# Fetching a layer's sub-weights by computed row numbers, and spreading a norm's statistics over four slots

## The chip, the cores and the metric

The kernel runs on one core of one Trainium2 chip. The metric is the device time of one execution in microseconds (us), the median of several runs. All values are fp32. The engines are named as the profile names them: PE is TensorE's matmuls and PEld its weight loads, DVE is VectorE, ACT is ScalarE, POOL is GpSimd, SP is the sync engine.

## The reference, cut to what matters

Each of 16 images (256 channels of 28 x 28) is group-normed, goes through two convolutions that are replaced by a lookup, and is added to itself.

```python
def amm_conv3x3(x, centroids, w_sub):                 # centroids (256,16,9), w_sub (256,9,256)
    p = patches(x)                                    # (B, 784, 256, 9)
    d = |p|^2 - 2 p.centroids + |centroids|^2         # (B, 784, 256, 16)
    attn = softmax(-d)
    lut = einsum('cks,cso->cko', centroids, w_sub)
    return einsum('bnck,cko->bno', attn, lut)

def block(v):
    out = relu(bn(amm_conv3x3(v, centroids1, wsub1)))
    out = bn(amm_conv3x3(out, centroids2, wsub2))
    return relu(se_layer(out) + v)

x = x + block(group_norm(x, G=32))                    # statistics over 8 channels x 784 points
```

The norm of an image is needed before that image's first layer and depends on nothing else, so its place in the program is free within limits. And `wsub2` is a weight: 256 x 9 rows of 256 floats, 2.36 MB, needed once, from layer 2's first tile on.

## The kernel before

The program is 32 stages (16 images, two layers) of 16 tiles, 512 tiles in all. I call the time of one tile a slot. A plan puts each small job (a norm step, a copy, a pattern write) into a slot, with a position within it: `SMALL` is in the middle of TensorE's work, `REST` at the end. Per tile TensorE makes 32 small logits matmuls, 32 small lookup matmuls and 8 or 10 large ones (128x384 or 128x400) with the sub-weights, as the profile counts them: it shows two for every matmul call in the code. VectorE transposes, GpSimd scales, ScalarE takes exponentials.

The kernel sorts channels by a key computed on the chip. `perm` is the sorting as a 0/1 matrix; a product with it on TensorE puts rows in sorted order. The second layer's sub-weights were sorted so, written to DRAM, and copied back in the layout that the large matmuls need:

```python
def load_part(ap, i):                       # 384 columns of wsub2, 393 KB
    t = tpool.tile([P, 832], F32, tag="z", name="part")[:, : NB * PART].rearrange(...)
    nc.sync.dma_start(t, ap[:, i * PART : (i + 1) * PART].rearrange("(b p) m -> p b m", p=P))
    parts[i] = t

def by_position(ps, rhs, m):                # L335: matmuls of 128 x m
    for v in range(NB):
        for b in range(NB):
            nc.tensor.matmul(ps[:, v, :m], lhsT=perm[:, b, v * P : (v + 1) * P], rhs=rhs[:, b],
                             start=(b == 0), stop=(b == NB - 1))

def sort_ws2(i):
    t = parts.pop(i)
    ps = pair()
    by_position(ps, t, PART)
    r = tpool.tile([P, 832], F32, tag="z", name="part")[...]
    nc.vector.tensor_copy(r, ps[:, :, :PART])
    nc.gpsimd.dma_start(view(d_ws2, i * PART, ...), r)

def place_ws2(i, t, j):                     # 16 copies back, and 8 more in place_tail
    p = 32 * i + 16 * t + 8 * j
    nc.sync.dma_start(ws[1][p : p + 8, : 2 * NQ], view(d_ws2, (NRT * j + 4 * t + i) * 9 * C, ...))

# ... in the plan:
for i in range(9 * C // PART):              # six parts
    plan.at(3 + i, REST, load_part, wsub2, i)
    plan.at(4 + i, REST, sort_ws2, i)
moves = [(place_wd2, ...) ...]              # 18 moves of the codes
moves += [(place_cw2, ...) ...]             # 32 moves of the codes
moves += [(place_ws2, ...) ...]             # 16
moves += [(place_tail, ...) ...]            # 8
for i, (f, *a) in enumerate(moves):
    plan.at(6 + i // 3, REST, f, *a)
```

The norm takes six slots: statistics of the image's two halves of channels, a matmul that averages them over each group, GpSimd's squared deviation `dv` of each channel's mean from its group's, a second matmul, and the two apply steps:

```python
def gn_stats(b, k):
    ...
    for i in range(2):
        nc.vector.bn_stats(st[:, i, :], xs[b][:, k, i * (HW // 2) : (i + 1) * (HW // 2)])   # L428
    nc.vector.bn_aggr(gst[b][:, k, :], st)

def gn_mean(b):
    nc.tensor.matmul(ps, lhsT=gmat, rhs=mv..., start=True, stop=True)     # L434
    nc.scalar.copy(gm..., ps)
    nc.gpsimd.tensor_sub(dv, mv[:, :, 0], gm[:, :, 0])
    nc.gpsimd.tensor_mul(dv, dv, dv)                                      # L439

def gn_var(b):
    nc.tensor.matmul(ps, lhsT=gmat, rhs=dv, start=True, stop=True)        # L445
    ...

def norm(self, b, t):
    self.at(t, REST, gn_stats, b, 0)
    self.at(t + 1, REST, gn_stats, b, 1)
    self.at(t + 2, SMALL, gn_mean, b)
    self.at(t + 3, SMALL, gn_var, b)
    self.at(t + 4, REST, gn_apply, b, 0)
    self.at(t + 5, REST, gn_apply, b, 1)

# ... in the plan, t being the first slot of the image's first layer:
n0 = 3 if b == 1 else t - 2 * NS - 3
plan.at(n0 - (4 if b == 1 else 2), REST, load_x, b, x[b])
plan.norm(b, n0)
```

## Time and profile before

| | before |
|---|---|
| median of 3 runs | 2895.39 us (2892.28 to 2902.37) |
| span of the profiled run | 2894.4 us |
| TensorE busy / idle | 2797.8 / 96.6 us |
| start of tile 4, 10, 34 | 60.3, 118.6, 277.6 us |
| tiles 44 to 480 (steady part) | 2350.3 us, 172.5 per two stages |

Where a tile starts is read by counting the logits matmuls in the timeline.

The first line to read is the chain of work that ended last, followed back from the end, as shares of the span by engine (from the page of the kernel before):

```profile
PE 77%; DMA 9%; POOL 6%; issue 4%; DVE 3%; ACT 0%; SPq 0%; POOLq 0%; DVEq 0%; ACTq 0%
```

TensorE carries three quarters of it. The other quarter is what TensorE waited for, and what those engines had waited for before; it is not TensorE's idle time, which is only 96.6 us. The chain leaves the bound engine only where that engine stopped.

One of the stops that come with every image, first on VectorE's timeline, then on TensorE's. The columns are the start, the duration, the engine and line, the operation with its tiles, the number of instructions, and in brackets the idle time before it and what ended it:

```profile
690.97 1.04 DVE L428 BATCH_NORM_STATS2 gn_st<-xt 128x6 f32<-128x392 f32 x2 [1.85 <-DMA xt<-in_x]
...
692.17 1.94 DVE L658 STREAM_TRANSPOSE nt<-pair 128x832 f32<-128x832 f32 x2
```

The other stop, on TensorE and on GpSimd, for another image:

```profile
1216.44 0.93 PE L578 MATMUL pair<-pt,wd 19*32 19x384 f32 x32
...
1221.07 0.38 PE L445 MATMUL pair<-gn_dv,gmat 128*128 128x2 f32 x2 [1.28 <-POOL gn_dv L439]
```

```profile
1220.83 0.19 POOL L439 TENSOR_TENSOR gn_dv<-gn_dv 128x2 f32<-128x2 f32 x1
```

GpSimd gets to the deviation behind its scaling work of that slot and ends it 4.58 us after the slot's first matmul (1216.44 to 1221.02). TensorE was there after 3.35 us. The first line also shows that an undisturbed set of 32 logits matmuls takes 0.93 us.

This is the view of windows (length of the stretch, then busy time and instructions of PE, PEld, DVE, ACT and POOL, then the granted clock, DMA share and GB/s):

```profile
1557.00:1560.60 3.60, 3.60 (x13) 1.85 (x6) 3.10 (x6) 0.84 (x1) 2.40 (x3) 0.54 0.60 215
```

### The profile page before, as it was taken

The numbers are of one execution on the slowest core, as the hardware profiler recorded it, in microseconds if no ns is written. First come the engines' busy times: TensorE is split into PE (matmuls) and PEld (weight loads), VectorE is DVE, ScalarE is ACT, GpSimd is POOL, SyncE is SP. The second block draws the span as 40 slices with busy tenths as digits, with TensorE's granted clock in tenths as the row PEclk, the third lists the DMA queues.
The fourth block names the chain that finished last, engine by engine and source line by source line (L and its number), as shares of the span: only waits on it lengthen the run. The fifth ranks groups of instructions, "written<-read, shape, count | busy, mean of one in ns | idle before, by whom it ended". The sixth has DMA issues, their size and how long they took to land.

```text
span 2894.4 us, 94782 instructions
## 1 busy us (share of the span) xinstructions
PE 2797.8 (97%) x39834; PEld 1105.5 (38%) x39834; DVE 2258.5 (78%) x2770; ACT 1090.3 (38%) x1595; POOL 1766.8 (61%) x2577
## 2 busy tenths in 40 slices
PE   6998999999999999999999999999999999999996
PEld 3433333333333333333333333333333333333332
DVE  4575888787877878788787877878788787878885
ACT  2332343433434343343433434343343434333332
POOL 3564675666756566675656656566665656656653
PEclk9999999999999999999999999999999999999998
DMA  8776878867767676776767767686776767774651
GB/s 230 193 181 173 208 219 207 221 159 212 192 173 200 153 220 173 198 200 154 217 161 202 190 177 191 158 224 163 216 191 163 204 156 215 185 186 119 154 134 57
DMA packets 296643, 530.27 MB, mean 183 GB/s; under 512 B 94240, under 2 KB 251632, under 8 KB 296208
## 3 DMA queue, kind: packets, MB, share of 16 engines
q0 software_dynamic: 51616, 269.48, 34.8%
q1 hardware_dynamic: 244592, 254.65, 34.5%
q8 instruction: 315, 5.16, 0.8%
q14 instruction: 120, 0.98, 0.1%
HBM read 269.96 MB, written 254.05 MB: 181 GB/s over the span
## 4 chain that ended last, share of the span: by engine, by line
PE 77%; DMA 9%; POOL 6%; issue 4%; DVE 3%; ACT 0%; SPq 0%; POOLq 0%; DVEq 0%; ACTq 0%
PE acc L710 49%; PE pair L578 15%; PE pair L646 13%; DMA xt<-in_x 4%; DMA pt<-pat 3%; POOL k L674 2%; POOL total L686 1%; DVE nt L658 1%; POOL pat L479 1%; POOL tail L680 1%; DVE rc L664 1%; DVE gn_st L428 1%; DMA pat<-side 1%; PE pair L335 1%; DMA part<-in_wsub 0%
## 5 line engine op out<-in xcount | busy, mean ns | idle before, releaser
L710 PE MATMUL acc<-q,ws 128*128 128x384 f32 (+1 forms) x4096 | 1648.1, 520 | 2.3 <-ACT y L732 2.3
L674 POOL TENSOR_TENSOR k<-nt,rc 128x832 f32<-128x832 f32 (+1 forms) x512 | 802.5, 1567 | 1079.0 <-DVE rc L664 1058.9
L658 DVE STREAM_TRANSPOSE nt<-pair 128x832 f32<-128x832 f32 (+1 forms) x1024 | 978.9, 994 | 524.6 <-PE pair L646 405.2
L636 ACT ACTIVATE e<-pair 128x800 f32<-128x800 f32 (+1 forms) x1024 | 789.5, 821 | 1414.7 <-PE pair L578 1368.9
L710 PEld LDWEIGHTS acc<-q,ws 128*128 128x128 f32 x4096 | 699.0, 190 | 900.3 <-issue 578.9
L578 PE MATMUL pair<-pt,wd 19*32 19x384 f32 (+2 forms) x18432 | 575.6, 501 | 33.7 <-DVE nt L658 18.1
L692 DVE STREAM_TRANSPOSE q<-k 128x832 f32<-128x832 f32 (+1 forms) x512 | 488.9, 955 | 0.8 <-POOL k L674 0.8
L646 PE MATMUL pair<-e,cw 32*32 32x384 f32 (+1 forms) x16384 | 485.1, 501 | 0.3 <-DVE nt L658 0.2
L664 DVE RECIPROCAL rc<-nt 128x104 f32<-128x104 f32 (+1 forms) x512 | 398.7, 779 | 17.6
L578 PEld LDWEIGHTS pair<-pt,wd 19*32 19x32 f32 (+1 forms) x18432 | 141.7, 103 | 379.0 <-issue 279.4
L680 POOL TENSOR_TENSOR tail<-nt,rc 128x104 f32<-128x104 f32 (+1 forms) x512 | 236.7, 462 | 0.0
L646 PEld LDWEIGHTS pair<-e,cw 32*32 32x32 f32 x16384 | 119.9, 103 | 290.2 <-issue 146.5
L710 PE MATMUL acc<-qt,ws 128*128 128x400 f32 (+1 forms) x512 | 221.9, 515 | 0.0
L686 POOL TENSOR_TENSOR total<-total,nt 128x96 f32<-128x96 f32 (+1 forms) x448 | 197.3, 440 | 0.0
L479 POOL DMA_DIRECT2D pat<-side x274 | 184.4, 673 | 3.4 <-ACT side L468 3.0
L686 POOL TENSOR_TENSOR total<-total,rc 128x96 f32<-128x96 f32 (+1 forms) x448 | 176.3, 394 | 0.0
L710 PEld LDWEIGHTS acc<-qt,ws 128*128 128x128 f32 x512 | 91.9, 192 | 101.1 <-issue 52.8
L602 DVE TENSOR_REDUCE mx<-z 128x48 f32<-128x768 f32 (+1 forms) x128 | 120.6, 942 | 0.0
L597 DVE STREAM_TRANSPOSE z<-pair 128x768 f32<-128x768 f32 (+1 forms) x128 | 118.1, 961 | 0.1
L479 POOL DMA_DIRECT2D pat<-im x136 | 91.8, 675 | 0.0
L732 ACT ACTIVATE y<-acc,bnsh,bnsc 128x384 f32<-128x384 f32 (+1 forms) x64 | 43.4, 678 | 86.9 <-PE acc L710 81.8
L544 POOL TENSOR_TENSOR y<-y,xt 128x392 f32<-128x392 f32 x60 | 65.9, 1099 | 10.4 <-ACT y L540 10.4
(109 smaller groups left out, 738.8 us busy)
## 6 DMA issues: line engine op xcount, KB each, us to landing
pat<-side POOLq DMA_DIRECT2D x232, 588.0 KB, 5.9
pt<-pat SPq DMA_DIRECT2D x1024, 112.5 KB
pt<-pat SPq DMA_DIRECT2D x1024, 108.0 KB
pat<-im POOLq DMA_DIRECT2D x116, 588.0 KB, 6.0
xt<-in_x POOLq DMA_DIRECT2D x32, 784.0 KB, 8.9
out_dram<-y POOLq DMA_DIRECT2D x16, 784.0 KB, 6.3
pat<-side POOLq DMA_DIRECT2D x24, 300.0 KB, 6.2
pat<-side POOLq DMA_DIRECT2D x18, 288.0 KB, 5.5
```

The lines of the kernel that those rows point to most:

```text
L479: eng.dma_start(view(pat, (ROWS * p0 + 9 * k + 3 * dx) * HW + px, [[ROWS * HW, m], [HW, 3], [1, n]]), bass.AP(v.tensor, v.offset, [list(v. ...
L578: nc.tensor.matmul(ps[t // 2][c : c + 32, t % 2, :n], lhsT=wd[l][32 * i : 32 * i + rows, 4 * u["m"] + t, :], rhs=u["pt"][32 * i : 32 * i + ...
L602: nc.vector.tensor_reduce(u["mx"][:, 2 * v : 2 * v + 2].rearrange("p t (j b) -> p t b j", j=2)[:, :, :nb], u["z"].pop(0)[:, : 64 * nb].rea ...
L636: nc.scalar.activation(e[:, :, :n], ps[:, :, :n], AF.Exp, scale=2.0)
L646: nc.tensor.matmul(u["nm"][t // 2][32 * i : 32 * i + 32, t % 2, :n], lhsT=cw[l][c : c + 32, 4 * u["m"] + t, :], rhs=es[t // 2][c : c + 32, ...
L658: nc.vector.transpose(nt[:, :nb, 2 * v : 2 * v + 2].rearrange("p b t r -> p t b r"), ps[:, :, : 32 * nb].rearrange("p t (b r) -> p t b r", ...
L664: nc.vector.reciprocal(rc[:, : 8 * nb], u["nt"][:, :, SUM])
L674: nc.gpsimd.tensor_tensor(q[:, :nb].rearrange("p b (a s) -> p (b a) s", s=8), nt[:, :, :8], rc.unsqueeze(2).to_broadcast([P, 8 * nb, 8]), ...
L680: nc.gpsimd.tensor_tensor(tails[key][:, :nb, 8 * (m % 4) : 8 * (m % 4) + 8], nt[:, :, 8].rearrange("p (b a) -> p b a", a=8), rc.rearrange( ...
L686: nc.gpsimd.tensor_add(t[:, : 8 * nb], t[:, : 8 * nb], v)
L692: nc.vector.transpose(q[:, :, : 32 * nb].rearrange("p h (b r) -> p h b r", r=32), u.pop("k")[:, :nb].rearrange("p b (h r) -> p h b r", h=2),)
L710: nc.tensor.matmul(accs[key][:, :n], lhsT=ws[l][:, 2 * m + h if h < 2 else 2 * NQ + m // 4, o * P : (o + 1) * P], rhs=u["q"][h][:, :n], st ...
```

## The change

The intent has two parts. First, the sub-weights need not be sorted as data. It is enough to know which channel sits at which position; then the rows can be fetched from the input straight to their places. The change sends the channel numbers through the same sorting product as the batch-norm vectors (`order`), spreads them over partitions with four small matmul calls against constant tables (`where`), multiplies by 9 and adds the tap number, and so has a row number for each of 128 partitions and 18 columns (`src`). Eighteen indirect DMAs from GpSimd, one in each of slots 6 to 23, fetch 128 rows of 1 KB each. The six loads, 48 matmuls, six VectorE copies, six stores and 24 copies back are gone.

Second, the norm: an image is loaded four slots ahead of its first statistics, the four statistics come one to a slot, the two small matmuls stand two slots apart. The apply steps keep their slots.

```diff
-    def load_part(ap, i):
-        ...
-    def sort_ws2(i):
-        ...
-    def place_ws2(i, t, j):
-        ...
-    def place_tail(i, j):
-        ...
+    def find_rows():
+        t = wh.pop()                                   # the constant tables, loaded in slot 2
+        stack = t[:, 4 * P : 4 * P + NLT]
+        ps = bank()[:, :NLT]
+        for c0, c1, part in ((0, 2 * NQ, 0), (2 * NQ, NLT, 1)):
+            for b in range(NB):
+                by = small.tile([P, NLT], F32, name="row_by")
+                nc.vector.tensor_scalar_mul(by[:, c0:c1], stack[:, c0:c1], order[:, b : b + 1])
+                nc.tensor.matmul(ps[:, c0:c1], lhsT=t[:, (2 * part + b) * P : (2 * part + b + 1) * P],
+                                 rhs=by[:, c0:c1], start=(b == 0), stop=(b == NB - 1))
+        nc.vector.tensor_scalar(src[:, : 2 * NQ], ps[:, : 2 * NQ], 9.0, t[...], op0=ALU.mult, op1=ALU.add)
+        nc.vector.tensor_scalar(src[:, 2 * NQ :], ps[:, 2 * NQ :], 9.0, 8.0, op0=ALU.mult, op1=ALU.add)
+
+    def fetch_ws2(g):
+        nc.gpsimd.indirect_dma_start(
+            out=ws[1][:, g], out_offset=None, in_=wsub2.rearrange("c (s o) -> (c s) o", s=9),
+            in_offset=bass.IndirectOffsetOnAxis(ap=src[:, g : g + 1], axis=0),
+        )
 # ... norm:
-            self.at(t, REST, gn_stats, b, 0)
-            self.at(t + 1, REST, gn_stats, b, 1)
-            self.at(t + 2, SMALL, gn_mean, b)
-            self.at(t + 3, SMALL, gn_var, b)
-            self.at(t + 4, REST, gn_apply, b, 0)
-            self.at(t + 5, REST, gn_apply, b, 1)
+            for n, (k, i) in enumerate((k, i) for k in range(NB) for i in range(2)):
+                self.at(t - 7 + n, REST, gn_stats, b, k, i)
+            self.at(t - 3, SMALL, gn_mean, b)
+            self.at(t - 1, SMALL, gn_var, b)
+            for k in range(NB):
+                self.at(t + k, REST, gn_apply, b, k)
 # ... plan:
-            n0 = 3 if b == 1 else t - 2 * NS - 3
-            plan.at(n0 - (4 if b == 1 else 2), REST, load_x, b, x[b])
+            n0 = 7 if b == 1 else t - 2 * NS + 1
+            plan.at(n0 - (8 if b == 1 else 11), REST, load_x, b, x[b])
-    for i in range(9 * C // PART):
-        plan.at(3 + i, REST, load_part, wsub2, i)
-        plan.at(4 + i, REST, sort_ws2, i)
-    moves = [...]
+    plan.at(2, REST, load_where)
+    plan.at(4, REST, find_rows)
+    for g in range(NLT):                               # 18
+        plan.at(6 + g, REST, fetch_ws2, g)
 # (the moves of the codes keep their order, at two or three to a slot)
```

## The prediction

> **What bounds the kernel now.** I read the page's busy rows and its 40 slices first, then TensorE's waits in the steady part, then VectorE's waits in the same stretch, then the first 300 us by waits, groups and windows.
>
> ```profile
> PE 2797.8 (97%) x39834; PEld 1105.5 (38%) x39834; DVE 2258.5 (78%) x2770; ACT 1090.3 (38%) x1595; POOL 1766.8 (61%) x2577
> ...
> PE   6998999999999999999999999999999999999996
> ```
>
> TensorE is busy 2798 of 2894 us: it is the bound, and only its idle time (96.6 us), its work, or its clock can be won. The program has 32 stages (16 images, two layers) of 16 tiles; I call the time of one tile a slot. Counting the logits matmuls (32 per tile) in the timeline, two stages take 172.4 us in the steady part, so a slot takes 5.4 us. Where the idle time lies:
>
> ```profile
> PE pair L445 <- POOL gn_dv L439: 16.6, 13, 1.3
> PE pair L578 <- DVE nt L658: 14.6, 12, 2.0
> ```
>
> These are TensorE's waits from 300 to 2700 us (sum, times, longest): nearly all the idle time of the steady part, and both come once per image, 13 and 12 times. The first is the norm's second small matmul, one slot after the first, waiting for GpSimd's deviation. The second has its cause one engine further back, in VectorE's waits of the same stretch:
>
> ```profile
> DVE gn_st L428 <- DMA xt<-in_x: 22.9, 13, 2.7
> ```
>
> The norm's statistics are asked for two slots after their image's load is issued, and VectorE stands in order before them; the transposes behind them free the PSUM pair late, and TensorE stops. In three images the stop also costs clock: the window view of 1557 to 1560.6 us has a granted clock of 0.54, and so do 1731 to 1734.6 (0.55) and 2250 to 2253.6 (0.53), against 1.00 around them.
>
> The start (TensorE's wait list of 40 to 120 us, then groups of the first 220 us, then windows):
>
> ```profile
> PE pair L335 <- DMA part<-in_wsub: 8.5, 1, 8.5
> ...
> L335 PE MATMUL pair<-part,sort_sb 128*128 128x384 f32 x48 | 18.8, 540 | 8.5 <-DMA part<-in_wsub 8.5
> ...
> 66.00:70.00 4.00, 0.24 (x1) 0.00 (x0) 3.04 (x6) 0.00 (x0) 2.52 (x4) 0.88 1.02 321
> 70.00:74.00 4.00, 0.00 (x0) 0.00 (x0) 0.00 (x0) 0.00 (x0) 0.00 (x0) 0.50 0.92 337
> ```
>
> Sorting the second layer's sub-weights costs 48 matmuls of 128x384 on TensorE, and the first waits 8.5 us for its load while the DMA engines are full (shares 1.02 and 0.92, third column from the end being the clock). In that idle the clock falls to 0.50. The second rough place:
>
> ```profile
> PE pair L578 <- DMA pt<-pat: 5.8, 5, 3.8
> PE pair L578 <- DMA pt<-dm: 3.7, 1, 3.7
> ```
>
> These are TensorE's waits of 200 to 320 us: at slots 27 to 33, where layer 2 starts, the patch loads come late. The sync engine's timeline there shows 24 copies of the sorted weights back into SBUF in the same queue, between the patch loads (from 197 to 264 us).
>
> **What the Trainium skill says.** "TensorE: Matmul & The Clock Gate", Part 1: an idle window throttles the array to half rate until it has been busy again for a window of 3.4 us. The trace agrees: 0.50 after the 8.5 us idle, and 3.4 us of half clock in each of the three stretches above. "DMA: Bandwidth & Descriptors", section "Issuing engines are not separate DMA queues": all DMAs share the same 16 engines. The trace agrees, as far as the 92 to 102% share with two queues active goes. Section "Issuing engine by pattern" there: indirect transfers go through GpSimd. There is none in this trace; its plain DMA issues on GpSimd take 0.65 to 0.76 us each. "GPSIMD Engine Reference", section 7: many small reads, for example one per gather index, cost about 102 cycles each without overlap. No trace here shows it; it feeds a rival below.
>
> **The change part by part.**
>
> 1. *Norm's statistics and the earlier load, steady part.* The load is now issued four slots ahead of its first statistics (21 us; a load lands in about 9 to 10.5 us by the xt view), so VectorE no longer waits. The four statistics of 0.54 us go one to a slot, and the mean and variance matmuls stand two slots apart, so GpSimd's deviation is long done. Removed: 16.6 + 14.6 = 31.2 us, and three times 3.4 us at half clock, 3 x 1.7 = 5.1 us. TensorE is the bound, so this lies on the path. The apply steps and pattern writes keep their slots. I take 34 of the 36.3.
>
> 2. *The sort of the sub-weights off TensorE, slots 4 to 10.* Tile 4's logits start at 60.3 us and tile 10's at 118.6: 58.3 us for six slots. Without the sort a slot here is two groups of small matmuls (0.86 each) and 9 of about 0.37, 5.05 us: 6 x 5.05 = 30.3. The difference, 28, is 18.8 us of sort, 8.5 of wait and the rest clock. Not all comes back: the row numbers need four small matmuls (about 0.3 us each) and six VectorE operations, and VectorE is free of tile 4 only at 68 us while TensorE is done at 66.2, so some 3.5 us go there; and the DMA engines stay full to about 72 us with pattern writes and the 512 KB code load, so GpSimd's scale, which waited for the sorted codes' write until 75.1, still waits to about 73. I take 20.
>
> 3. *The 18 gathers on GpSimd, slots 6 to 23.* GpSimd's base per slot is 1.52 + 0.43 + 0.43 + 0.38 = 2.8 us. Pattern writes add 1.0 in slots 9 to 16 (1.5 x 0.66) and 1.3 in slots 20 to 23. I estimate a gather of 128 rows at 1.3 us, twice a plain issue (0.66). That makes 5.1 to 5.4 us against a slot of 5.05: at the brim. In slots 9 to 17, with the squares (2.2) and the norm (2.0), it is about 9 x 5.2 + 4.2 = 51 us, where the kernel before took 57.5 less one sort of 2.6 = 55. So GpSimd becomes the local limit and leaves me 2 to 3 us there, including the 2.65 us wait for the second image's load at 144 us.
>
> 4. *DMA traffic.* Gone: 2.36 MB read in, 2.36 written sorted, 2.36 read back. New: 2.36 gathered and 0.27 of tables. Saved: 4.5 MB, and none of it in the slots where layer 2 starts. From slot 26 (208.7 us) to slot 34 (277.6) the kernel took 68.9 us; eight slots and two extra logits groups at the steady 84.7 per 16 slots would be about 43. Of the excess 26, I take half as due to weight copies ahead of patch loads and to the half clock after those waits; the rest is the pattern chain itself, which stays. 12 us.
>
> Sum: 34 + 20 + 2.5 + 12 = 68 us; 2895 - 68 = 2827, and I say **2828**.
>
> **The rivals.**
>
> *A: GpSimd becomes the bound in the start.* If a gather costs 3 us, slots 9 to 17 and 20 to 23 run about 1.8 us long and the others 0.8: 13 x 1.8 + 5 x 0.8 = 27 us back, gain 41, 2854. At the skill's 102 cycles per index and its 1.2 GHz a gather would be 128 x 102 / 1.2 GHz = 10.9 us (an estimate from that page): 18 of them would take GpSimd to 14 us a slot, 9 more than TensorE's, +160 us, so about 2990. For: GpSimd has only about 2 us free per slot. Against: plain issues with more than 128 descriptors take 0.66 to 0.76 us, so descriptors are not built at 85 ns each.
>
> *B: the first wait is replaced.* TensorE idled at 66 to 75 us while the DMA engines were at 92 to 102%. If patch loads of tiles 5 to 8 or the write of the sorted codes hold it instead, part 2 falls from 20 to about 10, and part 4 may fall to 4 since the chain from layer 1's last output to layer 2's patches is unchanged. That makes about 2845.
>
> *C: the steady stops move.* With both gone, the next limit could be VectorE (79% there) or the transfers. For it: little. DMA share is 0.72 and the load moves to a place with no other image's load. If half the stops stayed as other waits, 2845.
>
> **Range and chances.** The steady part is firm (30 to 37 us), the start soft (10 to 45). Both low: 2855 to 2862. Both high: 2805. Range 2803 to 2862. Two per cent is 58 us, a line at 2838; I am 10 us below it with a spread of about 22, so faster 0.66, same 0.30, slower 0.04 (the 10.9 us gather).
>
> **What would show it right or wrong.** Steps 1: the two wait lines and the statistics' wait vanish from 300 to 2700 us, and two stages take 170 us. Step 2: tile 10 starts at 95 to 104 us, no wait on a weight load. Step 3: the gathers' mean time on GpSimd near 1.3 us, and VectorE waiting somewhat more for GpSimd in slots 9 to 23. Step 4: waits for patches at 180 to 280 us under 5 us. The prediction is wrong if gathers take over 3 us each, if TensorE's idle in the first 300 us stays near 40 us with other names, or if the steady stops come back under another releaser.

## More of the kernel before

```profile
691.11 0.90 PE L578 MATMUL pair<-pt,wd 19*32 19x400 f32 x16
693.23 0.91 PE L578 MATMUL pair<-pt,wd 19*32 19x400 f32 x16 [1.22 <-DVE nt L658]
```

VectorE stands 1.85 us for the image (`xt`), then makes the statistics, and only then the transposes that free a PSUM pair. TensorE needs that pair for the second half of a tile's logits and stops for 1.22 us in the middle of them. Look also at the durations: 16 matmuls took 0.90 us and the other 16 took 0.91 us.

## The result

The changed kernel took 2816.1 us (median of 3 runs, 2812.3 to 2816.25) against 2895.39 us, a ratio of 0.9718 with a 95% interval of 0.9687 to 0.9748: faster. The outputs are right. A ratio here is the mean time of one kernel's fast runs over that of the other's of the same rounds, so it is not quite the ratio of the medians.

The busy row, TensorE's slices, and the chain that ended last, from the page of the changed kernel:

```profile
PE 2756.0 (98%) x39794; PEld 1090.2 (39%) x39794; DVE 2252.0 (80%) x2772; ACT 1086.5 (39%) x1595; POOL 1782.1 (63%) x2589
...
PE   6999999999999999999999999999999999999996
...
PE 92%; DVE 3%; POOL 2%; DMA 2%; issue 1%; ACT 0%; SPq 0%; DVEq 0%; POOLq 0%; ACTq 0%
```

TensorE's fourth slice, where layer 2 starts, has gone from 8 to 9. The chain now stays on TensorE for 92% of the span; DMA has 2% of it where it had 9, GpSimd 2 where it had 6. The span fell by 79.6 us (2894.4 to 2814.8), of which 37.8 are idle time of TensorE (96.6 to 58.8) and 41.8 are busy time. That busy time fell by so much is the first surprise: the sort's matmuls were only 18.8 us of it. Another 19.0 us are the logits matmuls, the same 18432 before and after, which went from 575.6 to 556.6 us in the groups of the two pages; the third experiment shows why.

By place, in us:

| stretch | before | after | saved | predicted |
|---|---|---|---|---|
| up to tile 4 | 60.3 | 62.0 | -1.7 | |
| tiles 4 to 10 | 58.3 | 37.7 | 20.6 | 20 |
| tiles 10 to 26 | 90.2 | 91.9 | -1.7 | 2.5 |
| tiles 26 to 34 | 68.9 | 50.1 | 18.8 | 12 |
| tiles 34 to 44 | 53.8 | 53.6 | 0.2 | |
| tiles 44 to 480 | 2350.3 | 2305.6 | 44.7 | 34 |
| tile 480 to the end | | | -1.3 | |
| span | 2894.4 | 2814.8 | 79.6 | 68 |

TensorE's waits of the steady part, 290 to 2620 us (sum, times, longest), after:

```profile
PE pair L441 <- DVE gn_mv L436: 4.2, 13, 0.3
```

Both stops that the prediction shows are gone, and VectorE's wait for the image with them. In their place the mean matmul waits 0.3 us per image for the last statistics. They come in the slot just before it, as they did in the kernel before, but the mean now stands one slot earlier, where four large matmuls are ahead of it and not six, so TensorE gets there sooner. The stretch that ran at half clock runs at full clock:

```profile
66.00:70.00 4.00, 2.29 (x24) 1.05 (x8) 3.77 (x7) 0.40 (x2) 3.75 (x7) 1.00 1.02 312
70.00:74.00 4.00, 4.00 (x42) 2.25 (x43) 0.58 (x4) 1.22 (x2) 0.00 (x0) 0.55 0.87 297
1557.00:1560.60 3.60, 3.60 (x65) 1.55 (x40) 3.57 (x5) 0.79 (x2) 3.48 (x5) 1.00 0.75 171
```

The first two lines are the stretch that stood idle before, waiting for the first part to sort. TensorE now works for all of 70 to 74 us, but at half clock (0.55). Why, its timeline tells, and the list of waits of the first 120 us beside it:

```profile
69.88 1.34 PE L384 MATMUL pair<-row_by,where 128*128 128x16 f32 x8 [1.71 <-issue]
71.15 1.58 PE L585 MATMUL pair<-pt,wd 19*32 19x384 f32 x32
```

```profile
PE pair L585 <- DMA pt<-pat: 6.1, 1, 6.1
...
PE pair L384 <- issue: 1.7, 1, 1.7
```

The matmuls that find the row numbers wait 1.7 us (their operand comes from VectorE, which is behind with tile 4 and starts on it at 69.59 us), and the clock then stays at half from 70.5 to 77.3 us; the 32 logits matmuls at 71.15 take 1.58 us instead of 0.93. The 6.1 us wait for patches lies before tile 4, where the kernel before had one of 3.5 us.

TensorE's waits of 200 to 320 us, where layer 2 starts:

```profile
PE acc L717 <- ACT im L729: 2.3, 1, 2.3
PE pair L585 <- DMA pt<-pat: 0.4, 1, 0.4
```

The patch waits of 5.8 and 3.7 us before have come down to 0.4. And the gathers, as a group of GpSimd's in the first 220 us (busy and mean ns of one, then idle time before and what ended it), and in the view of the tile of row numbers (shortest, median, longest ns, first and last start, then the time to landing):

```profile
L394 POOL DMA_INDIRECT ws<-in_wsub,src x18 | 18.4, 1022 | 4.7 <-issue 4.3 <-DMA cw<-dc 0.3
```

```profile
L394 POOL DMA_INDIRECT ws<-in_wsub,src x18: 976/1024/1078, 91.0 to 189.0; - x18
...
DMA to landing us min/median/max: 4.9/7.2/10.8
```

A gather holds GpSimd for 1.02 us, with about 0.25 us (4.7 / 18) of issue ahead of it.

### The profile page after: what moved, and what is told of

Read it like the earlier page. It is cut to its first block, busy times and chain, and to the rows that moved or that the text cites.

```text
span 2814.8 us, 94692 instructions
## 1 busy us (share of the span) xinstructions
PE 2756.0 (98%) x39794; PEld 1090.2 (39%) x39794; DVE 2252.0 (80%) x2772; ACT 1086.5 (39%) x1595; POOL 1782.1 (63%) x2589
## 2 busy tenths in 40 slices
DMA packets 292787, 525.83 MB, mean 187 GB/s; under 512 B 94096, under 2 KB 247552, under 8 KB 292352
## 4 chain that ended last, share of the span: by engine, by line
PE 92%; DVE 3%; POOL 2%; DMA 2%; issue 1%; ACT 0%; SPq 0%; DVEq 0%; POOLq 0%; ACTq 0%
PE acc L717 58%; PE pair L585 17%; PE pair L653 15%; DVE nt L665 1%; POOL k L681 1%; DMA pt<-pat 1%; DVE q L699 0%; DMA pat<-side 0%; DVE rc L671 0%; PE pair L319 0%; DMA out_dram<-y 0%; POOL pat L486 0%; PE pair L514 0%; POOL total L693 0%; DVE gn_st L434 0%
## 5 line engine op out<-in xcount | busy, mean ns | idle before, releaser
L585 PE MATMUL pair<-pt,wd 19*32 19x384 f32 (+2 forms) x18432 | 556.6, 501 | 11.4 <-DMA pt<-pat 8.2
```

The lines of the kernel that those rows point to most:

```text
L585: nc.tensor.matmul(ps[t // 2][c : c + 32, t % 2, :n], lhsT=wd[l][32 * i : 32 * i + rows, 4 * u["m"] + t, :], rhs=u["pt"][32 * i : 32 * i + ...
```

## The experiments

The main theory was that the two parts add, each with the sizes of the table above. The rivals are told with each run. Sizes by place come from the one profiled run of each kernel. Runs of the kernel before scatter by up to 20 us (2887 to 2907), and one trace does not show where in the run that falls, so a difference of 5 us in the start of a single trace is no evidence by itself. With the new norm the steady part repeats within 2 us (2305.5 to 2307.4 us in the changed kernel and four of its variants). With the old norm it doesn't: it took 2346.9, 2350.3, 2353.0 and 2357.1 us in the four traces that have it unchanged (the gathers alone, the kernel before, the copies first, the sort later), with 2, 3, 4 and 5 stretches of half clock in them. So the 44.7 us of the table stand for 41 to 52, and the three stretches that the prediction counted are one trace's number.

Two stretches of the start are far outside the scatter. Tiles 4 to 10 took 58.3 to 59.4 us in the four traces with the sort in its old slots, and 34.9 to 41.6 in the eight without the sort's work. Tiles 26 to 34 took 66.7 to 73.8 us in the four traces with the 24 copies in their old place, and 48.1 to 51.1 in the other ten.

### The norm alone

All of the norm's hunks of the change, on the kernel before; the sort stays.

```diff
+            for n, (k, i) in enumerate((k, i) for k in range(NB) for i in range(2)):
+                self.at(t - 7 + n, REST, gn_stats, b, k, i)
+            self.at(t - 3, SMALL, gn_mean, b)
+            self.at(t - 1, SMALL, gn_var, b)
 # ...
+            plan.at(n0 - (8 if b == 1 else 11), REST, load_x, b, x[b])
```

> The kernel before with the norm's part of the change alone (earlier load, statistics in four slots, mean and variance two slots apart); the sort stays on TensorE. Theory: the two parts add up. The norm is worth 45 us in the steady part (the slot times of the two traces differ by that from slot 44 to slot 480) and 2 to 4 us for the second image in the start: about 2847 us, 1.7% faster, and from slot 96 on two stages take 169.2 us as in the changed kernel, while tile 34 still starts near 275 us. Rival: the parts need each other, for instance the steady stops fall away because the start no longer leaves the transfers behind; then this run keeps over half of the steady stops and stays above 2870 us.

Measured: 2845.76 us against 2903.3 in the same rounds, ratio 0.9805 (0.9781 to 0.9829). The steady part took 2306.9 us, as in the whole change. TensorE's waits there:

```profile
PE pair L434 <- DVE gn_mv L429: 4.5, 13, 0.6
...
```

What follows: the norm part alone gives the whole steady gain. The profiled run was this kernel's slowest (2856.89 us), so its start, where tile 34 came 6 us later than in the kernel before, says little.

### The gathers alone

The other hunks: the norm stays as it was.

```diff
+    plan.at(2, REST, load_where)
+    plan.at(4, REST, find_rows)
+    for g in range(NLT):
+        plan.at(6 + g, REST, fetch_ws2, g)
-    (loads, sorts and copies back)
```

> The changed kernel with the old norm: the gather's part alone. Theory: tile 34 starts near 243 us (36 us early) as in the changed kernel, the steady part keeps its stops (172.4 to 173 us for two stages), total about 2859 us, 1.2% faster. Rival: the start's gain came in good part from the norm of the second and third image; then tile 34 starts at 250 us or later and the total is above 2868 us.

Measured: 2860.48 us, ratio 0.9866 (0.9837 to 0.9895). Tile 34 started at 243.3 us (277.6 before, 241.6 with the whole change), and the steady part kept both stops:

```profile
PE pair L452 <- POOL gn_dv L446: 16.6, 13, 1.3
PE pair L585 <- DVE nt L665: 13.1, 13, 2.0
```

What follows: the gain of the start, 34 us by tile 34, comes with the gathers' part alone, whose hunks also set the moves of the codes two to a slot; that was not tried apart. The product of the two ratios is 0.967, that of the whole change 0.972. The single parts come out larger than the whole, by half a per cent, but the intervals overlap: within them the parts add.

### Only the earlier load of the image

One number on the kernel before. It separates the two stops of the norm.

```diff
-            plan.at(n0 - (4 if b == 1 else 2), REST, load_x, b, x[b])
+            plan.at(n0 - (4 if b == 1 else 7), REST, load_x, b, x[b])
```

> The kernel before with one thing changed: the norm's image load is issued five slots earlier from the third image on. Theory: the stop behind the statistics is worth 2.25 us per image (the slot times), more than the 1.2 us of idle that the wait list shows, since half of the interrupted logits group and the half clock after it count as busy: 13 x 2.25 and some 3 us for the third image, about 2863 us. Rival (the sum of the prediction): idle and half clock alone, 14.6 + 5.1 us, about 2875 us. The wait for the deviation, 1.3 us per image, stays in both.

Measured: 2865.62 us, ratio 0.9879 (0.9855 to 0.9904). The steady part took 2321.6 us, 28.7 less than before, while the prediction had counted 14.6 of waits and 5.1 of clock for this stop, 19.7. The deviation's wait stands at the head of the list of 290 to 2620 us as before (16.6 us in 13 times); below it the wait on `nt` is gone and only these are left:

```profile
...
PE pair L578 <- DMA pt<-dm: 1.0, 3, 0.5
PE pair L578 <- DMA pt<-pat: 0.5, 1, 0.5
```

What follows: the stop was worth 2.2 us per image (28.7 / 13), not the 1.2 that the list of waits shows. Against the other traces of the old norm the 28.7 would be 25 to 36, and by the ratio of all runs the gain is 35 us (28 to 42), the start included; 19.7 is below all of these. The timeline shown above of the kernel before says where the rest is: from 691.11 to the next operation at 694.06 the two halves of a tile's logits took 2.95 us, where an undisturbed set takes 0.86 to its successor (1216.44 to 1217.30). That is 2.1 us lost, and 0.9 of them are counted as busy, because each half of 16 matmuls shows about the duration of the whole 32. Counted so, the 13 interrupted sets of the kernel before took 25.7 us more than undisturbed ones (the median set of the steady part takes 0.88), of which 14.7 are idle and 11.0 busy; in the trace of this run no set was interrupted. In the page's groups the busy time of the logits matmuls fell accordingly, first the kernel before, then this one:

```profile
L578 PE MATMUL pair<-pt,wd 19*32 19x384 f32 (+2 forms) x18432 | 575.6, 501 | 33.7 <-DVE nt L658 18.1
```

```profile
L578 PE MATMUL pair<-pt,wd 19*32 19x384 f32 (+2 forms) x18432 | 565.7, 501 | 17.2 <-DMA pt<-pat 11.7
```

The same 18432 matmuls are busy 9.9 us less.

### The two small matmuls side by side again

On the changed kernel, the second matmul one slot earlier. The prediction had said that two slots between the matmuls take the deviation's wait away, so this should have brought it back.

```diff
-            self.at(t - 1, SMALL, gn_var, b)
+            self.at(t - 2, SMALL, gn_var, b)
```

> The changed kernel with the variance's matmul moved back to the slot right after the mean's. Theory: TensorE waits for GpSimd's deviation again, about 1.3 us for each of 14 images: 16 to 18 us more than the changed kernel, about 2833 us. Rival: the statistics are ready earlier in their slot now, so GpSimd is done in time and the time stays at 2816 us.

Measured: 2819.9 us, ratio 0.9717 (0.9693 to 0.974); the changed kernel had 0.9718. The theory fell. The steady part took 2310.6 us, 5.0 more than with the whole change, and the wait came back at a sixth of its size:

```profile
...
PE pair L452 <- POOL gn_dv L446: 2.7, 13, 0.2
...
```

TensorE's timeline in one such slot, then GpSimd's:

```profile
1164.03 0.95 PE L585 MATMUL pair<-pt,wd 19*32 19x400 f32 x32
...
1168.29 0.38 PE L452 MATMUL pair<-gn_dv,gmat 128*128 128x2 f32 x2 [0.21 <-POOL gn_dv L446]
```

```profile
1168.04 0.19 POOL L446 TENSOR_TENSOR gn_dv<-gn_dv 128x2 f32<-128x2 f32 x1
```

GpSimd ends the deviation 4.20 us after the slot's first matmul, a little sooner than the 4.58 before. But TensorE gets there after 4.05 us instead of 3.35, because this slot has six large matmuls ahead of the `SMALL` position and the next one four. So it is not only the distance that matters but also the slot in which the second matmul stands.

### The norm's statistics and mean one slot later

The follow-up, to tell slot from distance. The second matmul keeps the changed kernel's slot, and the mean comes right before it.

```diff
-                self.at(t - 7 + n, REST, gn_stats, b, k, i)
-            self.at(t - 3, SMALL, gn_mean, b)
+                self.at(t - 6 + n, REST, gn_stats, b, k, i)
+            self.at(t - 2, SMALL, gn_mean, b)
```

> The changed kernel with statistics, mean one slot later and variance where it is, so mean and variance stand in the two slots in which they stood before (adjacent, the second in a slot with four lookup matmuls ahead of it), while the statistics stay in four slots and the load stays early. The run before this showed that adjacency one slot earlier costs only 0.2 us per image. Theory: what made the wait was the slot, TensorE reaching the variance 3.4 us into its slot and GpSimd 4.6 us into it; so the wait of 1.3 us per image is back and the time is about 2832 us, 16 us over the changed kernel. Rival: splitting the statistics is what got VectorE and so GpSimd there in time; then 2816 to 2820 us.

Measured: 2824.83 us, ratio 0.9751 (0.9732 to 0.9771). The steady part took 2319.7 us, 14.1 more than with the whole change, and the wait was back in full:

```profile
PE pair L452 <- POOL gn_dv L446: 16.5, 13, 1.3
...
```

The whole time was only 9 to 10 us longer than the changed kernel's (8.7 by the medians, 9.6 by the ratios), not the 16 of the theory; the start of this trace, by tile 34, was 4.3 us shorter.

What follows: adjacent in slots 15 and 16 (counted by the tiles of two stages) costs 16.5 us of waiting, adjacent in 14 and 15 costs 2.7, two apart costs none. The change is free of the wait because of its distance, and would have been nearly free of it with the earlier slot alone. The two stops together, 28.7 and about 14 to 16, are the 44.7 us of the steady part. Nothing is left for the spread of the statistics over four slots. This run has it and the run with only the earlier load doesn't; load, mean and second matmul stand in the same slots in both, and the steady part took 2319.7 and 2321.6 us. So the spread itself earned nothing that these traces can separate.

### The copies back ahead of the codes

On the kernel before, nothing removed: the 24 copies of sorted weights stand in the sync engine's queue before the 32 moves of codes, so that they are not among layer 2's patch loads.

```diff
     moves = [(place_wd2, j, s) for j in range(NCH) for s in range(9)]
-    moves += [(place_cw2, i, t, j) for j in range(NCH) for i in range(4) for t in range(4)]
     moves += [(place_ws2, i, t, j) for j in range(NCH) for i in range(4) for t in range(2)]
     moves += [(place_tail, i, j) for j in range(NCH) for i in range(4)]
+    moves += [(place_cw2, i, t, j) for j in range(NCH) for i in range(4) for t in range(4)]
```

> The kernel before with the 24 copies of the sorted weights issued ahead of the 32 small code copies (slots 12 to 20 instead of 22 to 30); nothing is taken away. Theory (step 4 of the prediction): the copies hold up the patch loads of layer 2's first tiles by their place in the queue, so tile 26 to tile 34 falls from 68.9 us to about 52, total about 2880 us. Rival: it is the volume of the sorted weights' traffic or the pattern chain; then those tiles keep at least 65 us and the total stays within 5 us of the kernel before, or the waits turn up in slots 12 to 20.

Measured: 2898.05 us, ratio 0.9996 (0.9969 to 1.0022), the same. But not in every stretch: tiles 26 to 34 took 48.8 us, as with the whole change (50.1), and tiles 10 to 26 took 99.4 where the kernel before took 90.2. In this trace, of one of its faster runs (2887.54 us), some 10 us of the 20 stay by tile 34, and the median time shows no gain. So the theory held for its stretch (about 52 us) and missed the total (2880 us); the rival had the total right, and waits in the earlier slots. Its waits of 30 to 290 us:

```profile
...
PE pair L578 <- DMA pt<-pat: 6.6, 3, 6.1
PE pair L578 <- DVE nt L658: 3.0, 1, 3.0
...
```

What follows: the 18.8 us of tiles 26 to 34 did come from the copies that stood among the patch loads; the moves of the codes, which took their place there, did no such harm. In their new place the copies cost about half as much in this trace, and the median time leaves no gain. Taking them out of the program is what made the gain stay; other places for them were not tried.

### The sort four slots later

On the kernel before, to ask whether its cost was the time at which it asked for its data. The loads stand three slots later and the sorts four, so each load is two slots ahead of its sort and not one.

```diff
-        plan.at(3 + i, REST, load_part, wsub2, i)
-        plan.at(4 + i, REST, sort_ws2, i)
+        plan.at(6 + i, REST, load_part, wsub2, i)
+        plan.at(8 + i, REST, sort_ws2, i)
```

> The kernel before with the six sorts in slots 8 to 13 and their loads in slots 6 to 11, two slots ahead, past the time when the DMA engines are full. Theory: of the 19 us that the gather gains by tile 10, the sort's matmuls are 15.5 us (6 x 2.58) and stay, the wait of 8.5 us and the half clock after it (3 to 5 us) go, less the wait for patches that then shows; tile 16 starts some 7 to 11 us earlier than 157.2 us, total about 2886 us. Rival: TensorE waits for the transfers there in any case; then tile 16 is within 3 us of 157.

Measured: 2903.65 us, ratio 1.0027 (0.9995 to 1.0059), the same. Tiles 4 to 10 took 13 us less, tiles 10 to 16 took 18 us more, so tile 16 started 5.6 us later than in the kernel before; theory and rival both missed that. The weight load no longer stops TensorE, others do (30 to 290 us):

```profile
PE pair L578 <- DMA pt<-pat: 12.5, 7, 5.2
PE pair L646 <- DVE part L358: 7.7, 2, 4.3
PE pair L445 <- POOL gn_dv L439: 6.2, 1, 6.2
...
```

What follows: this better time for the same work did not win the 20 us. What won them took work and traffic away.

### Plain loads in place of the gathers

On the changed kernel, and **wrong** (relative error 0.91): the sync engine loads the same number of rows without the row numbers, so GpSimd issues none of them. This measures what the 18 gathers cost GpSimd.

```diff
-        nc.gpsimd.indirect_dma_start(out=ws[1][:, g], out_offset=None, in_=..., in_offset=...)
+        nc.sync.dma_start(ws[1][:, g], wsub2.rearrange("c (s o) -> (c s) o", s=9)[g * P : (g + 1) * P])
```

> The changed kernel with each of the 18 gathers replaced by a plain load of 128 rows of the same size on the sync engine's queue, in the same slots; the result is wrong on purpose (unsorted rows). It takes 18.4 us of gathers off GpSimd and leaves bytes and slots. Theory: between 160 and 205 us the changed kernel's chain runs through GpSimd, whose pattern writes of slots 20 to 25 come late behind gathers; so tile 34 starts 3 to 6 us earlier than 241.6 us, total 2810 to 2813 us. Rival: the gathers are hidden behind TensorE; then tile 34 is within 1.5 us of 241.6, total 2816 us.

Measured: 2815.33 us, ratio 0.9723 (0.9704 to 0.9743). Tile 34 started at 239.1 us, 2.5 us sooner than with gathers, which one trace cannot tell from scatter. What follows: taking the gathers off GpSimd gains nothing that these runs can separate. The plain loads could cost something of their own on the sync engine's queue, which this run can't tell apart.

### The gathers two to a slot, from slot 5

The opposite of the run above: eight of the gathers are pressed into four slots.

```diff
-        plan.at(6 + g, REST, fetch_ws2, g)
+        plan.at(5 + g // 2 if g < 8 else 1 + g, REST, fetch_ws2, g)
```

> The changed kernel with the gathers two to a slot in slots 5 to 8 and then one to a slot to 18, so that GpSimd has none in slots 19 to 23, where the patterns of layer 2 are written. Theory: GpSimd's chain of 160 to 205 us gets shorter and tile 34 starts 2 to 4 us earlier than 241.6 us, total 2812 to 2814 us. Rival, which the plain loads made likelier: the gathers are hidden, and the total stays within 2 us of 2816.

Measured: 2816.08 us, ratio 0.9717 (0.9694 to 0.974). The start by tile 34 was 242.5 us, against 241.6. The rival held: moving the gathers to these slots changed nothing here.

### The sort's work put back, without its transfers

On the changed kernel: six times eight matmuls of 128x384 and a VectorE copy, in the slots in which the sort stood, on data already there and into a buffer that nothing reads. The result stays right. This splits the start's gain into work and traffic.

```diff
+    def sort_work():
+        t = ws[0].rearrange("p a c -> p (a c)")[:, : NB * PART].rearrange("p (b m) -> p b m", b=NB)
+        ps = pair()
+        by_position(ps, t, PART)
+        r = tpool.tile([P, 832], F32, tag="z", name="part")[:, : NB * PART].rearrange("p (b m) -> p b m", b=NB)
+        nc.vector.tensor_copy(r, ps[:, :, :PART])
 # ...
+    for i in range(6):
+        plan.at(4 + i, REST, sort_work)
```

> The changed kernel with the sort's compute put back without its transfers: in slots 4 to 9 TensorE does the same 48 matmuls of 128x384 on weights that lie in SBUF, and VectorE the six copies; nobody uses the result, so the output stays correct. It tells how much of the start's gain is TensorE work and how much is transfers. Theory: TensorE is the bound in slots 4 to 10, so 6 x 2.58 = 15.5 us come back there and stay: tile 10 near 115 us, total about 2832 us. Rival: after the two runs on the kernel before (copies first, sort later), the start is set by transfers, and work on TensorE is absorbed by shorter waits for patches at tiles 14 to 34; then tile 34 is less than 8 us late and the total is below 2824 us.

Measured: 2823.07 us, ratio 0.9744 (0.972 to 0.9768). Tile 10 started at 113.2 us, 13.5 later than in the changed kernel; at tile 34 the difference was 10.1, and in the whole time it is 7 us by the medians, some 7.5 by the ratios (0.9744 less 0.9718, of 2900). The theory had tile 10 about right and the rival the total; tile 34 lies between them. What follows: of the 16.5 us that the matmuls put back took in this trace (18.8 in the kernel before, where the first eight ran at half clock), 13.5 show where they stood, and 7 to 10 stay to the end; the stretch up to tile 34 took up the rest. The larger share of the 36 us that the start gained by tile 34 is therefore the removed waits and transfers and not the matmuls.

### The row numbers found one slot later

On the changed kernel, against the 1.7 us wait and its half clock: VectorE's scalings stay in slot 4, the four matmuls move to the middle of slot 5, and ScalarE takes the result out of PSUM.

```diff
-    plan.at(4, REST, find_rows)
+    plan.at(4, REST, scale_rows)
+    plan.at(5, SMALL, find_rows)
 # in find_rows:
-        ps = bank()[:, :NLT]
+        ps = spare()[:, :NLT]
+        row = small.tile([P, NLT], F32, name="row_of")
+        nc.scalar.copy(row, ps)
```

> The changed kernel with the row numbers found in two steps: VectorE scales in slot 4, TensorE's four matmuls follow in the middle of slot 5, copied out by ScalarE, so TensorE doesn't stand at the end of slot 4 for VectorE (1.7 us of wait and 1.3 us of matmuls in the trace, then 6.8 us at half clock). Theory: tile 10 starts 3 to 5 us earlier than 99.7 us and the total is 2811 to 2813 us. Rival: tile 5 waits for its patches at 70 us anyway; then tile 10 is within 1.5 us of 99.7.

Measured: 2812.72 us, ratio 0.9708 (0.9683 to 0.9732). In the trace tiles 4 to 10 took 34.9 us instead of 37.7, and the wait on the row numbers is gone. The time is the lowest median, but its interval and that of the changed kernel overlap almost wholly, so it cannot be called faster.

### Three improvements at once

The row numbers as in the run above, the gathers two to a slot, and the steady statistics one slot earlier, so that the mean matmul does not wait 0.3 us.

```diff
-                self.at(t - 7 + n, REST, gn_stats, b, k, i)
+                self.at(t - (7 if b == 1 else 8) + n, REST, gn_stats, b, k, i)
-        plan.at(6 + g, REST, fetch_ws2, g)
+        plan.at(5 + g // 2 if g < 8 else 1 + g, REST, fetch_ws2, g)
 # and find_rows as above
```

> The two edits above together, and the norm's statistics one slot earlier still (from the third image on), so that TensorE doesn't wait for the last of them (0.3 us per image, 4.2 us in all). Theory: 4 us from the statistics, 3 to 6 from the start: 2806 to 2809 us, 3.1% faster than the kernel before. Rival: the start's waits move, and only the 4 us of the statistics are left: 2812 us.

Measured: 2814.36 us, ratio 0.9702 (0.9678 to 0.9725), short of both the theory and the rival, and not to be told from the changed kernel. The steady part was the best of all, 2301.2 us, 4.4 less than the changed kernel's, with the mean's wait gone. The start gave 5 us back by tile 34 (246.6 against 241.6). GpSimd's timeline in slots 7 and 8, then ScalarE's and TensorE's:

```profile
83.10 1.11 POOL L402 DMA_INDIRECT ws<-in_wsub,src  x1 [0.18 <-issue]
84.51 0.98 POOL L402 DMA_INDIRECT ws<-in_wsub,src  x1 [0.30 <-issue]
...
89.80 0.24 POOL L468 TENSOR_SCALAR gn_nb<-gn_nb 128x2 f32<-128x2 f32 x1
```

```profile
90.07 1.04 ACT L473 ACTIVATE im<-xt,gn_nb,gn_rstd 128x784 f32<-128x784 f32 x1 [6.84 <-POOL gn_nb L468]
91.02 1.54 ACT L651 ACTIVATE e<-pair 128x800 f32<-128x800 f32 x2
```

```profile
91.88 1.53 PE L661 MATMUL pair<-e,cw 32*32 32x384 f32 x16 [2.63 <-ACT e L651]
```

The two gathers take GpSimd from 83.10 to 85.49 us, ahead of that slot's scaling and of the norm of image 1. So the norm's factor (`gn_nb`) comes at 89.80, where it came at 86.95 in the run above with the same row numbers and no gather there. ScalarE stands 6.84 us in order before its apply step (4.19 in the run above), its exponentials come late, and TensorE stops for 2.63 us. The clock then stays at half for 10.2 us (91.3 to 101.6). But the two gathers alone do not make the stop. In the run with the gathers two to a slot the same two stood ahead of the same norm (83.66 to 86.05 us), and the factor came at 90.35. But TensorE came to that place some 3.6 us later (91.99 us, not 88.38) and did not stop; its lookup set took 1.33 us instead of 0.93. So a gather stays hidden here as long as what stands behind it on GpSimd is not yet needed. A version with the later row numbers and the earlier statistics but one gather to a slot was not run; it would be some 4 us below the 2812.72 of the run above, an estimate from the steady part's 4.4 us.

## Why the prediction was right, point by point

The time of 2816.1 us lies in the predicted range, 12 us below the predicted 2828, and faster by over 2% was the likeliest class. The sum was 68 where the span fell by 79.6. The parts were less sure than the total: the one that the prediction called firm, 30 to 37 us for the steady part, came out at 44.7, outside, and it was the width given to the start (10 to 45, measured 36 by tile 34) that left room for it. By its steps:

**Step 1, the norm: the mechanism was right, the size was too small.** Both stops vanished, VectorE's wait for the image too, no half clock was left in the steady part, and the norm alone gives all of it. Two stages take 169.2 us, near the predicted 170. The term "14.6" was mis-sized: the runs give 28.7 (25 to 36, by the trace it is compared with) for that stop with its clock, not 19.7. The wait list holds only the idle time, and a stop in the middle of a set of 32 overlapped matmuls also costs about 0.9 us that counts as busy (11.0 us for the 13 sets, counted above, which covers the missing 9). Also, "the mean and variance matmuls stand two slots apart, so GpSimd's deviation is long done" was true but not the whole reason. Side by side, the two matmuls wait 16.5 us in one pair of slots and 2.7 in the pair before it. And the four statistics "one to a slot" had no part in it: with and without them the steady part differs by 1.9 us.

**Step 2, the sort off TensorE: right.** 20.6 us in tiles 4 to 10 for 20, no wait on a weight load, and tile 10 started at 99.7 us, in the predicted 95 to 104. The 3.5 us for the row numbers were there as a 1.7 us wait and a stretch of half clock of 6.8 us.

**Step 3, the gathers: wrong in a small thing.** A gather holds GpSimd for 1.02 us, not 1.3, but tiles 10 to 26 took 1.7 us more and not 2.5 less. VectorE did not wait more for GpSimd in slots 9 to 23, as foretold, but less (2.4 us, 8.1 before). In the trace of the changed kernel one tile there waits 1.7 us for its patches and the clock stays at half for 6.9 us after it (0.51 from 128.5 to 135.4 us). In the variants with the same norm and with gathers that stretch took between 88.3 us and 92.8 us, so 2.5 us is below what one trace can tell. Rival A, GpSimd as the bound, falls by the plain loads and the early gathers. Something like it came only in the last run, where two gathers stood ahead of image 1's norm and TensorE came early. One of its reasons is not in the traces: the plain issues do not have "more than 128 descriptors", they move 96 packets (a pattern write) to 128 (an image).

**Step 4, the traffic: right in its cause, mis-sized.** The prediction took half of an excess of 26 us; the runs show 18.8. The 84.7 us per 16 slots in that excess don't fit its own 172.4 per two stages, which gives 86.2 and an excess of 24. Nor is it so that none of the saved traffic was in those slots: the 24 copies back, 2.36 MB from 197 to 264 us, were, as its own reading of the sync engine's timeline says. The copies ahead of the patch loads were the cause in these slots, as their move alone shows. That they cost elsewhere when moved was not in the prediction. The bytes moved fell from 530.27 to 525.83 MB, 4.4 for the predicted 4.5.

**Rival B**, a wait in place of the first, came true in small at most: the patch wait before tile 4 is 6.1 us where it was 3.5, and tile 4 starts 1.7 us later. But it started at 60.9 to 61.7 us in the variants of the kernel before too, where nothing of this was changed, so that may be scatter. **Rival C**, steady stops that come back under another name, came to 4.2 us, and the last run, with the statistics one slot earlier, has no such wait.

What stays open: how the start's gain divides between waits and transfers once the work's 7 to 10 us are taken off. An experiment with the sort's transfers but without its matmuls was not run.

## What to carry to other kernels

A stop in the middle of a set of overlapped small matmuls cost here 1.75 times what the list of waits says (25.7 us for 14.7), so measure from the start of the set to its successor and not only the idle time. Before spreading jobs over more slots, look at which slot lets the waiting engine arrive late and the supplying engine early: one slot's move was here worth nearly as much as a slot of distance. And ask whether a transfer in the way can be taken out: moved within the same queue, it took back about half of what it gave in the one trace here, and the median time kept none of it.

## What the Trainium skill lacked or had wrong

- "GPSIMD Engine Reference", section 7, gives about 102 cycles for each small read that does not overlap; the prediction worked out 10.9 us for a gather of 128 rows from it as a rival. An indirect DMA of 128 rows of 1 KB held GpSimd for 0.98 to 1.08 us, 8 ns a row, with about 0.25 us of issue before it and 7.2 us (4.9 to 10.8) to landing. The figure, which the page gives for programs that run on GpSimd's own cores, does not carry over to these indirect DMAs, and no page that I read gives the cost of one.
- "TensorE: Matmul & The Clock Gate", Part 1, section "HAM oscillation — how this bites in real kernels", puts the rule as "no PE-idle gaps >~3.4µs." Read as a safe limit, it fails here: the clock fell to about half for 3.4 to 6.9 us after stops of 1.1 to 1.9 us (before: 1.94, 1.09 and 1.55 us in the steady part; after: 1.7 us at the row numbers and 1.7 us at a patch wait). So the three stretches, which the prediction counted as agreeing with the page, agree in their length of 3.4 us and not in the idle time ahead of them. Most stops of that length did nothing: of the 21 stops of 1.09 us or more in the steady part of the kernel before, 3 did so, all three in the middle of a set of logits matmuls, and the longest, 2.04 us, was not one of them.
